# A graph network in one launch: the count codes made in other steps, and the check of the edge order taken off VectorE

## The chip, the cores and the metric

The kernel runs on one core of a Trainium2 chip. The metric is the device time of one execution in microseconds (us); a time of the kernel is the median of several runs. The engines are named as the profile names them: PE (TensorE; PEld are its weight loads), DVE (VectorE), ACT (ScalarE), POOL (GpSimd) and SP (SyncE, which here only starts transfers).

## The reference

```python
h = jnp.maximum(_layernorm(x, axis=-1), 0.0)      # x: 6250 nodes x 256
def agg(h):                                       # 100,000 edges src -> dst, sorted by dst
    return jax.ops.segment_sum(h[src], dst, num_segments=N)
for l in range(3):
    h = x + agg(x)                                # here x is the layer's input
    h = relu(h @ W1s[l] + b1s[l]); h = relu(h @ W2s[l] + b2s[l])
    x = h @ W3s[l] + b3s[l]
h = x + agg(x)                                    # the head has cW1, cW2 (256 to 64), cW3
out = x_in + (relu(relu(h @ cW1 + cb1) @ cW2 + cb2) @ cW3 + cb3)
```

So there are four aggregations, each a sum of neighbours' rows, and a small dense network behind each.

## The kernel before, in words

The 6250 nodes make 49 tiles of 128. An aggregation is done for most of its work as a dense product: the adjacency counts are built once as matrices of small integers (`mats`, built by `build` with the matmuls of line 1254 from the two one-hot factors of line 1200), and every layer multiplies them with the node features (line 1937, `agg<-a,XY`). A part of the nodes, those of low degree, is summed by gathering rows one per edge (line 1622, on POOL's queue).

Ahead of all this stands a **preparation**, whose instructions are put out in an order that the Python code fixes (a manual schedule), by generators that a driver loop steps on in turn. Three of them matter here.

- `normed` does the layer norm and the first product, `z = relu(norm(x)) @ W1`, for the 49 tiles in 25 pairs (0 to 24; the last has one tile). It is a pipeline over steps s. In step s, in this order: `out(s-3)` copies the product of pair s-3 from PSUM to `zs` on DVE (line 1053), `high(s-4)` rounds it into `XY` on ACT (line 1058), `scale(s)` makes the normed rows `h` on ACT (line 1025), `turn(s-1)` transposes them on PE (`agg<-ident,h`, line 1034) and copies the result to `ht` on ACT (line 1037), `times(s-2)` multiplies on PE (`bp<-w,ht`, line 1046), and `low(s-4)` takes the rest `zs - XY` on POOL (line 1063; five of the pairs on DVE). `keep(s-5)` stores `zs` (SP). The products lie in two PSUM buffers, so the product of pair p can start only when `out(p-2)` has copied its buffer away.
- `look` finds the range of edges of each half tile, and near its end, in lines 823 to 850, does two things in one go: it turns the **count codes** `cT` (a field of 128 x 16 x 50 bf16 inside `clT`) into a place below 128 and a weight of 1 or 256 for an odd or even count (`odd`, written over `weigh`), and it makes the **check**: are the edges in order (`run`, 892 int32 a partition, compared with itself shifted by one), does a window hold all its edges, do the windows end in range. The findings go to the four columns of `wrong`; a matmul with ones adds them over the partitions (line 847), and two small DVE steps make the flag `good` of them, which the end of the program reads to choose a fallback.
- `ranking` sorts the nodes by degree, mostly on DVE (lines 892 to 977).

The driver counts half steps h of `normed` (two for each s) and steps `look` on after those in the tuple `LOOK`, whose last is 45: after the whole of step s = 22. There all of lines 823 to 850 is put out at once, behind `out(19)` and ahead of `turn(22)`. Each engine works its list strictly in that order.

Behind the preparation its memory is given back. The first instruction of the build, the ACT copy `pairs<-clT` (line 1188), waits for everything that used that memory, the last stores of `zs` among them.

Of the kernel before, what the change touches and what calls it, by code (L numbers as in the profile page):

```python
# [9 lines left out]
F32 = mybir.dt.float32  # L10
I32 = mybir.dt.int32
# [3 lines left out]
BF16 = mybir.dt.bfloat16  # L15
AF = mybir.ActivationFunctionType
OP = mybir.AluOpType
PSUM = bass.MemoryType.PSUM
DRAM = bass.MemoryType.DRAM
P = 128  # L20
# [400 lines left out]
def sorted_edges(  # L421
# [39 lines left out]
    nc = tc.nc  # L461
# [8 lines left out]
    GD = 4  # L470
    NSUB = 2 * NT
    GSUB = 64 // GD
    TWO = GD // 2
    HW = NT * TWO
    STEP = 64
# [7 lines left out]
    EC = 892  # L483
# [8 lines left out]
    U = NT - NS  # L492
# [50 lines left out]
    cT, weigh, loT = clT[:, 0], clT[:, 1], clT[:, 2]  # L543
# [149 lines left out]
    def look(pool):  # L693
# [5 lines left out]
        run = pool.tile([P, EC + 1], I32, name="run", bufs=1)  # L699
        nc.gpsimd.memset(run, FAR)  # L700
        both = pool.tile([P, EC], I32, name="both", bufs=1)
        nc.gpsimd.memset(both, 0)
        for e, t, m in ((dst, run, EC + 1), (src, both, EC)):
# [18 lines left out]
                                       op1=OP.bitwise_or)  # L722
# [8 lines left out]
        for h in range(2):  # L731
# [5 lines left out]
                                    op0=OP.is_lt, op1=OP.add, accum_out=half[:NSUB, h:h + 1])  # L737
# [6 lines left out]
        near_i = pool.tile([P, NEAR], I32, name="near_i", bufs=1)  # L744
# [18 lines left out]
        less = pool.tile([P, GSUB + 1], F32, name="less", bufs=1)  # L763
        junk2 = near_i.bitcast(BF16)[:, :NEAR]
        DV = 11
        for k in range(GSUB + 1 - DV):
            for q in range(2 * k, min(2 * k + 2, DV)):
                nc.vector.tensor_scalar(junk[:NSUB], near[:NSUB], float(GD * q), None,  # L768
                                        op0=OP.is_lt, op1=OP.add, accum_out=less[:NSUB, q:q + 1])
            q = DV + k  # L770
            nc.scalar.activation(junk2[:NSUB], near[:NSUB], AF.Sign, bias=edge[:NSUB, q:q + 1],
                                 accum_out=less[:NSUB, q:q + 1])
            yield
        nc.vector.tensor_scalar(less[:NSUB, DV:], less[:NSUB, DV:], -0.5, float(NEAR // 2),
                                op0=OP.mult, op1=OP.add)
# [20 lines left out]
        for q0 in range(0, GSUB, H):  # L796
# [4 lines left out]
            hi = pool.tile([P, H, P], I32, name="hi", bufs=1)  # L801
            nc.vector.tensor_scalar(hi[:NSUB], wd[:NSUB, cut, :], 7, None,
                                    op0=OP.arith_shift_right)
# [5 lines left out]
            for t, o in ((r, cT), (f, loT)):  # L809
                for i in range(0, H, 4):  # L810
# [6 lines left out]
                    if t is r:  # L817
# [2 lines left out]
            yield  # L820


        odd = weigh[:, :, :2 * U]
        nc.vector.tensor_scalar(odd, cT[:, :, :2 * U], float(2 * STEP), -1.0, op0=OP.is_ge,
                                op1=OP.mult)
        for t in range(1, GD, 2):
            nc.vector.scalar_tensor_tensor(odd, cT[:, :, :2 * U], float(t * STEP), odd,
                                           op0=OP.is_ge, op1=OP.add)
        nc.vector.scalar_tensor_tensor(cT[:, :, :2 * U], odd, float(-STEP), cT[:, :, :2 * U],
                                       op0=OP.mult, op1=OP.add)  # L830
        nc.vector.tensor_scalar(odd, odd, 255.0, 1.0, op0=OP.mult, op1=OP.add)
        wrong = pool.tile([P, 4], F32, name="wrong", bufs=1)
        nc.vector.memset(wrong, 0.0)
        down = pool.tile([P, EC], F32, name="both", bufs=1)
        nc.vector.tensor_tensor(down, run[:, 1:EC + 1], run[:, :EC], OP.is_lt)
        nc.vector.tensor_reduce(wrong[:, 0:1], down, axis=mybir.AxisListType.X, op=OP.max)
        size = pool.tile([P, GSUB], F32, name="size", bufs=1)
        nc.vector.tensor_tensor(size[:NSUB], less[:NSUB, 1:], less[:NSUB, :GSUB], OP.subtract)
        nc.vector.tensor_scalar(size[:NSUB], size[:NSUB], float(P), None, op0=OP.is_gt)
        nc.vector.tensor_reduce(wrong[:NSUB, 1:2], size[:NSUB], axis=mybir.AxisListType.X,  # L840
                                op=OP.max)
        nc.vector.tensor_scalar(wrong[:NSUB, 2:3], less[:NSUB, GSUB:], float(NEAR), None,
                                op0=OP.is_ge)
        nc.vector.scalar_tensor_tensor(wrong[:NSUB, 2:3], first[:NSUB, GSUB:], float(E),
                                       wrong[:NSUB, 2:3], op0=OP.is_lt, op1=OP.mult)
        bad = ps_m.tile([P, W], F32, name="ps")
        nc.tensor.matmul(bad[:1, :4], ones[:, 0:1], wrong, start=True, stop=True)
        total = pool.tile([1, 1], F32, name="total", bufs=1)
# [5 lines left out]
    def stored_later(pool):  # L854

        zero = pool.tile([P, C], F32, name="b3b", bufs=1)
        nc.gpsimd.memset(zero, 0.0)
        yield
        for t in tables:
            nc.sync.dma_start(out=t[N:N + PAD, :], in_=zero)  # L860
        nc.sync.dma_start(out=padded[0:E].rearrange("(o e) -> o e", o=16),
                          in_=src.rearrange("(o e) -> o e", o=16))
        nc.sync.dma_start(out=padded[E:E + KR].rearrange("(o e) -> o e", o=1),
                          in_=src[E - KR:E].rearrange("(o e) -> o e", o=1))
        yield
# [224 lines left out]
            yield  # L1090

    sums = ps_g.tile([P, W], F32, name="sums")
    LOOK = tuple(range(17, 33, 2)) + (45,)
    RANK = tuple(range(33, 42))
    LATER = (14, 24)

    with tc.manual_schedule():
        with tc.tile_pool(name="prep", bufs=2) as prep, tc.tile_pool(
            name="ps_t", bufs=2, space=PSUM
        ) as ps_t, tc.tile_pool(name="ps_z", bufs=2, space=PSUM) as ps_z:  # L1100
            cN = prep.tile([P, 2 * NS, GSUB], BF16, name="cN", bufs=1)
            looked = look(prep)
            ranked = ranking(prep)
            next(looked)
            rows = normed(prep, ps_t, ps_z)
            next(rows)
            make_identity(nc, ident)
            nc.vector.tensor_copy(ident_r, ident)
            nc.vector.memset(eps, EPS)
            turn_biases, (b1, b2, b3) = load_biases(prep)  # L1110
            ahead_w = fused(prep, [W3s[l] for l in range(NLAYER)],
                            [W1s[l + 1] for l in range(NLAYER - 1)] + [cW1])
            next(ahead_w)
            next(looked)
            for t, pattern, base in ((cols[:, :U * TWO], [[1, U], [2 * STEP, TWO]], NS),
                                     (cols[:, U * TWO:], [[1, NS], [2 * STEP, TWO]], 0),
                                     (lanes, [[1, P]], 0), (colf, [[1, P]], 0)):
                nc.gpsimd.iota(t, pattern=pattern, base=base, channel_multiplier=0,
                               allow_small_or_imprecise_dtypes=True)
            next(looked)  # L1120
            next(rows)
            turn_biases()
            next(ranked)
            next(ranked)
            for k in range(2 * NLAYER):
                next(looked)
                next(ahead_w)
                if k == 0:
                    next(rows)
                next(rows)  # L1130
                next(rows)
            next(looked)
            stores = stored_later(prep)
            for h, _ in enumerate(rows, 4 * NLAYER):
                if h % 2:
                    ask(2)
                if h in LOOK:
                    next(looked)
                if h in RANK:
                    next(ranked)  # L1140
                if h in LATER:
                    next(stores)
            assert next(ranked, 0) == 0 and next(looked, 0) == 0 and next(stores, 0) == 0

        work = ctx.enter_context(tc.tile_pool(name="work", bufs=1))
# [827 lines left out]
        with tc.tile_pool(name="hots", bufs=1) as hots, tc.tile_pool(  # L1973
            name="ats", bufs=1
        ) as ats, tc.tile_pool(name="rings", bufs=AHEAD + 2) as rings, tc.tile_pool(
            name="gath", bufs=9
        ) as gath, tc.tile_pool(name="nd", bufs=1) as nd, tc.tile_pool(
            name="ps_a", bufs=2, space=PSUM
# [96 lines left out]
```

## Time and profile before

| | before |
|---|---|
| median of 3 runs (lowest to highest) | 2008.25 us (2006.13 to 2008.99) |
| the profiled execution: its time, its span | 2005.61 us, 2003.8 us |
| busy in the span: PE, PEld, DVE, ACT, POOL | 94%, 74%, 52%, 54%, 65% |
| chain that ended last: PE, DVE, DMA | 83%, 6%, 4% |
| preparation's last product ends, build begins | 130.5 us, 133.8 us |

The span runs from the first instruction to the last, and the 1.8 us between it and the execution's time lie around it. Starts in the profile are in us from the span's start. In a row of the timeline the first number is the start, the second how long the group took, and the bracket at the end, if there is one, tells how long the engine sat idle ahead of it and what ended that. In the rows of windows each engine's busy time stands ahead of the number of its instructions, and PEclk is the TensorE clock that was granted, as a share of full speed.

### The profile page before, as it was taken

The numbers are of one execution on the slowest core, as the hardware profiler recorded it, in microseconds if no ns is written. First come the engines' busy times: TensorE is split into PE (matmuls) and PEld (weight loads), VectorE is DVE, ScalarE is ACT, GpSimd is POOL, SyncE is SP. The second block draws the span as 40 slices with busy tenths as digits, with TensorE's granted clock in tenths as the row PEclk, the third lists the DMA queues.
The fourth block names the chain that finished last, engine by engine and source line by source line (L and its number), as shares of the span: only waits on it lengthen the run. The fifth ranks groups of instructions, "written<-read, shape, count | busy, mean of one in ns | idle before, by whom it ended". The sixth has DMA issues, their size and how long they took to land.

```text
span 2003.8 us, 29049 instructions
## 1 busy us (share of the span) xinstructions
PE 1885.4 (94%) x9236; PEld 1472.8 (74%) x9236; DVE 1034.1 (52%) x2213; ACT 1077.4 (54%) x2164; POOL 1311.1 (65%) x1444
## 2 busy tenths in 40 slices
PE   5955999999999899999999999999999999999997
PEld 3734766777777787777789777777788877777775
DVE  7877887677756343333344353333345354343433
ACT  4734776776766564444445464444445564455442
POOL 2526666766766556777777466676777466777775
PEclk9876999999999999999999999999999999999999
DMA  5523656665656475555656575564657576565553
GB/s 167 176 74 115 201 176 197 203 210 183 206 187 212 155 241 163 173 182 162 185 169 206 168 248 168 159 198 149 187 168 230 160 216 202 184 200 171 180 176 106
DMA packets 252333, 361.40 MB, mean 180 GB/s; under 512 B 33352, under 2 KB 206312, under 8 KB 252154
## 3 DMA queue, kind: packets, MB, share of 16 engines
q1 hardware_dynamic: 188160, 190.34, 30.0%
q0 software_dynamic: 61952, 166.87, 27.5%
q10 hardware_dynamic: 2058, 2.25, 0.4%
q8 instruction: 74, 1.21, 0.3%
q14 instruction: 89, 0.73, 0.1%
HBM read 292.33 MB, written 67.40 MB: 180 GB/s over the span
## 4 chain that ended last, share of the span: by engine, by line
PE 83%; DVE 6%; DMA 4%; issue 2%; POOL 2%; ACT 1%; SPq 0%; DVEq 0%; ACTq 0%; POOLq 0%
PE agg L1937 66%; PE ps L1514 6%; PE ps L1417 6%; DMA rows<-table,idxN 2%; PE bp L1254 2%; POOL rows L1622 1%; DVE hi L1200 1%; PE pt L1685 1%; PE bp L1046 1%; DVE lo L1200 1%; POOL lane L1743 1%; PE ps L1431 1%; DMA wd<-joined,starts 0%; DVE ws L768 0%; DMA lane<-padded,at 0%
## 5 line engine op out<-in xcount | busy, mean ns | idle before, releaser
L1937 PE MATMUL agg<-a,XY 128*128 128x512 f32 (+1 forms) x6272 | 1513.1, 393 | 15.4 <-DVE a L1910 6.9
L1622 POOL DMA_INDIRECT rows<-table,idxN x1121 | 1087.1, 970 | 473.9 <-PE agg L1937 211.0
L1937 PEld LDWEIGHTS agg<-a,XY 128*128 128x128 f32 x6272 | 1146.7, 189 | 249.2 <-issue 12.7
L1908 ACT CAST a<-at 128x512 fp32r<-128x512 uint8 (+1 forms) x1249 | 709.4, 602 | 237.9 <-PE agg L1937 226.8
L1658 DVE TENSOR_TENSOR sums<-sums,rows 128x512 f32<-128x512 f32 x477 | 332.1, 696 | 499.6 <-DMA rows<-table,idxN 444.8
L1910 DVE CAST a<-at 128x512 fp32r<-128x512 uint8 (+1 forms) x312 | 141.7, 460 | 171.4 <-PE agg L1937 147.8
L1262 ACT CAST at<-bp 128x392 uint16<-128x392 f32 x227 | 110.3, 489 | 128.0 <-PE bp L1254 122.2
L1417 PE MATMUL ps<-h,w 128*128 128x512 f32 (+2 forms) x336 | 135.3, 546 | 0.0
L1514 PE MATMUL ps<-w,h 128*128 128x256 f32 x588 | 133.7, 379 | 0.0
L1200 DVE TENSOR_TENSOR lo<-lanes,pairs 128x512 bf16<-128x512 bf16 x256 | 107.1, 424 | 45.1 <-PE bp L1254 44.3
L1254 PEld LDWEIGHTS <-lo 128*128 128x128 bf16 x1028 | 57.5, 103 | 96.8 <-DVE lo L1200 41.9
L1254 PE MATMUL bp<-hi,lo 128*128 128x98 bf16 x1028 | 95.2, 219 | 33.4 <-DVE lo L1200 27.1
L1514 PEld LDWEIGHTS ps<-w,h 128*128 128x128 f32 x588 | 111.2, 190 | 15.9
L596 POOL DMA_INDIRECT table<-zz,ids x72 | 72.9, 1013 | 66.3 <-DVE zz L1519 48.1
L1654 ACT COPY sums<-rows 128x512 f32<-128x512 f32 x74 | 43.8, 593 | 122.5 <-DMA rows<-table,idxN 101.1
L1420 ACT ACTIVATE h<-ps,bias 128x512 f32<-128x512 f32 (+2 forms) x84 | 51.7, 636 | 95.1 <-PE ps L1417 95.1
L1417 PEld LDWEIGHTS ps<-h,w 128*128 128x128 f32 x336 | 63.0, 193 | 52.6 <-issue 37.8
L1519 DVE TENSOR_TENSOR zz<-ps,w 128x512 f32<-128x512 f32 (+1 forms) x81 | 50.5, 639 | 96.0 <-PE ps L1514 89.3
L1693 ACT ACTIVATE h<-pt,bias 128x256 f32<-128x256 f32 (+1 forms) x84 | 33.1, 446 | 124.3 <-PE pt L1685 124.2
L1344 DVE TENSOR_TENSOR XY<-back,XY 128x256 fp32r<-128x256 f32 x138 | 55.1, 423 | 46.9 <-ACT XY L1343 46.0
L1951 ACT ACTIVATE h<-agg,bias 128x512 f32<-128x512 f32 (+1 forms) x60 | 37.6, 671 | 73.3 <-PE agg L1937 73.1
L1200 DVE TENSOR_TENSOR hi<-hi,pairs 128x784 bf16<-128x784 bf16 x128 | 72.6, 568 | 4.4
(235 smaller groups left out, 952.0 us busy)
## 6 DMA issues: line engine op xcount, KB each, us to landing
at<-mat SPq DMA_DIRECT2D x140, 448.0 KB
mat<-at SPq DMA_DIRECT2D x32, 784.0 KB
at<-mat SPq DMA_DIRECT2D x62, 336.0 KB
rows<-table,idxN POOLq DMA_INDIRECT x1121
back<-table SPq DMA_DIRECT2D x138, 128.0 KB
table<-zz SPq DMA_DIRECT2D x35, 256.0 KB
at<-mat SPq DMA_DIRECT2D x63, 112.0 KB
own<-zz SPq DMA_DIRECT2D x55, 128.0 KB
```

What stands on the lines that cost most here:

```text
L596: got = nc.gpsimd.indirect_dma_start(out=ap, out_offset=bass.IndirectOffsetOnAxis(ap=ids[:, b:b + 1], axis=0), in_=sb, in_offset=None)
L1200: nc.vector.tensor_tensor(o, values, which[:, :, None, :].to_broadcast(shape), op)
L1254: mm = nc.tensor.matmul(bp[:, m * HW:(m + 1) * HW], lo[:, m, :], hi[:, m, :], start=(i == 0), stop=(i == len(sets) - 1))
L1262: nc.scalar.copy(o, v)
L1344: later(1, lambda: nc.vector.tensor_tensor(XY[:, j:j + m, C:], z[:, :m, :], XY[:, j:j + m, :C].bitcast(F32), OP.subtract))
L1417: mm = nc.tensor.matmul(ps[:, :w], weights[l][0][:, c, i * P:(i + 1) * P], h1[:, c, :w], start=(c == 0), stop=(c == KC - 1))
L1514: mm = nc.tensor.matmul(o, h2[0][:, c, nodes], w3[:, c, :], start=(c == 0), stop=(c == KC - 1))
L1622: got = nc.gpsimd.indirect_dma_start(out=t[:, c % 2, :], out_offset=None, in_=tables[self.l][:, :], in_offset=bass.IndirectOffsetOnAxis(ap ...
L1658: nc.vector.tensor_tensor(sums, sums, rows.rearrange("p h c -> p (h c)"), OP.add)
L1908: nc.scalar.copy(o, v)
L1910: nc.vector.tensor_copy(o, v)
L1937: mm = nc.tensor.matmul(agg[c][:, :w], XY[:, j, o:o + P], a[:, :w], start=(i == 0 and half == 0), stop=(i == NT - 1 and half == 1))
```

## The change

Four things change, all in the preparation.

1. The codes are made of seven DVE steps in place of five: four `tensor_scalar` and three `tensor_tensor`, none of which takes a scalar and two tensors at once. The result is the same. One of them writes a small tile of its own (`upper`, under the name `hi`).
2. The edge order is checked by a subtraction on POOL (`rise`) and a Relu on ACT that adds up the falls, in place of a comparison and a reduction on DVE. The clearing of `wrong` and the subtraction `size` go to POOL as well.
3. `look` yields twice more. `LOOK` ends in (43, 45): the codes come a step earlier, behind `out(18)`; the check stays behind step 22.
4. The product with `wrong` and the two steps that make `good` come behind the whole of `normed`.

```diff
-        odd = weigh[:, :, :2 * U]
-        nc.vector.tensor_scalar(odd, cT[:, :, :2 * U], float(2 * STEP), -1.0, op0=OP.is_ge,
+        code, odd = cT[:, :, :2 * U], weigh[:, :, :2 * U]
+        nc.vector.tensor_scalar(odd, code, float(2 * STEP), float(-2 * STEP), op0=OP.is_ge,
                                 op1=OP.mult)
-        for t in range(1, GD, 2):
-            nc.vector.scalar_tensor_tensor(odd, cT[:, :, :2 * U], float(t * STEP), odd,
-                                           op0=OP.is_ge, op1=OP.add)
-        nc.vector.scalar_tensor_tensor(cT[:, :, :2 * U], odd, float(-STEP), cT[:, :, :2 * U],
-                                       op0=OP.mult, op1=OP.add)
-        nc.vector.tensor_scalar(odd, odd, 255.0, 1.0, op0=OP.mult, op1=OP.add)
+        nc.vector.tensor_tensor(code, code, odd, OP.add)
+        upper = pool.tile([P, GSUB, 2 * U], BF16, name="hi", bufs=1)
+        nc.vector.tensor_scalar(upper, odd, -1.0, None, op0=OP.mult)
+        nc.vector.tensor_scalar(odd, code, float(STEP), float(-STEP), op0=OP.is_ge, op1=OP.mult)
+        nc.vector.tensor_tensor(code, code, odd, OP.add)
+        nc.vector.tensor_tensor(code, code, upper, OP.add)
+        nc.vector.tensor_scalar(odd, odd, -255.0 / STEP, 1.0, op0=OP.mult, op1=OP.add)
+        yield
         wrong = pool.tile([P, 4], F32, name="wrong", bufs=1)
-        nc.vector.memset(wrong, 0.0)
-        down = pool.tile([P, EC], F32, name="both", bufs=1)
-        nc.vector.tensor_tensor(down, run[:, 1:EC + 1], run[:, :EC], OP.is_lt)
-        nc.vector.tensor_reduce(wrong[:, 0:1], down, axis=mybir.AxisListType.X, op=OP.max)
+        nc.gpsimd.memset(wrong, 0.0)
+        rise = pool.tile([P, EC], I32, name="both", bufs=1)
+        nc.gpsimd.tensor_tensor(rise, run[:, 1:EC + 1], run[:, :EC], OP.subtract)
+        rest = near_i.bitcast(BF16)[:, :EC]
+        nc.scalar.activation(rest, rise, AF.Relu, scale=-1.0, accum_out=wrong[:, 0:1])
         size = pool.tile([P, GSUB], F32, name="size", bufs=1)
-        nc.vector.tensor_tensor(size[:NSUB], less[:NSUB, 1:], less[:NSUB, :GSUB], OP.subtract)
+        nc.gpsimd.tensor_tensor(size[:NSUB], less[:NSUB, 1:], less[:NSUB, :GSUB], OP.subtract)
...
+        yield
         bad = ps_m.tile([P, W], F32, name="ps")
         nc.tensor.matmul(bad[:1, :4], ones[:, 0:1], wrong, start=True, stop=True)
...
-    LOOK = tuple(range(17, 33, 2)) + (45,)
+    LOOK = tuple(range(17, 33, 2)) + (43, 45)
...
+            next(looked)
             assert next(ranked, 0) == 0 and next(looked, 0) == 0 and next(stores, 0) == 0
```

Lines behind the change are 1 to 5 higher in the changed kernel: line 1053 is 1057 there, 1034 is 1038, 1046 is 1050, 1063 is 1067, 847 is 851. On DVE, before, near the end of the preparation (`zs<-bp` are the copies of `out`, here of pairs 18 and 19; the rows on `clT` are the codes, the rest is the check):

```order
L977 CAST what<-bits 128x24x3
L1053 COPY zs<-bp 128x512 x2
L824 TENSOR_SCALAR clT<-clT 128x16x50
L827 SCALAR_TENSOR_TENSOR clT<-clT 128x16x50 x2
L829 SCALAR_TENSOR_TENSOR clT<-clT 128x16x50
L831 TENSOR_SCALAR clT<-clT 128x16x50
L833 MEMSET wrong 128x4
L835 TENSOR_TENSOR both<-run 128x892
L836 TENSOR_REDUCE wrong<-both 128x1
L838 TENSOR_TENSOR size<-less 98x16
L839 TENSOR_SCALAR size<-size 98x16
L840 TENSOR_REDUCE wrong<-size 98x1
```

The same place on DVE in the changed kernel:

```order
L981 CAST what<-bits 128x24x3
L1057 COPY zs<-bp 128x512
L824 TENSOR_SCALAR clT<-clT 128x16x50
L826 TENSOR_TENSOR clT<-clT 128x16x50
L828 TENSOR_SCALAR hi<-clT 128x800
L829 TENSOR_SCALAR clT<-clT 128x16x50
L830 TENSOR_TENSOR clT<-clT 128x16x50
L831 TENSOR_TENSOR clT<-clT,hi 128x16x50
L832 TENSOR_SCALAR clT<-clT 128x16x50
L1057 COPY zs<-bp 128x512
L842 TENSOR_SCALAR size<-size 98x16
L843 TENSOR_REDUCE wrong<-size 98x1
```

The codes now stand between `out(18)` and `out(19)`, four rows of the check are gone from DVE, and the two steps that make `good` follow only behind `out(24)`.

On PE, before, the last products of the norm (`agg<-ident,h` is `turn`, `bp<-w_0_131,ht` is `times`) and the check's product among them; the two rows ahead of it are `turn(21)` and `times(20)`:

```order
L1034 MATMUL agg<-ident,h 128x128 x4
L1046 MATMUL bp<-w_0_131,ht 128x256 x4
L847 MATMUL ps<-wrong,ones 1x4
L1034 MATMUL agg<-ident,h 128x128 x4
L1046 MATMUL bp<-w_0_131,ht 128x256 x4
L1034 MATMUL agg<-ident,h 128x128 x4
L1046 MATMUL bp<-w_0_131,ht 128x256 x4
L1034 MATMUL agg<-ident,h 128x128 x2
L1046 MATMUL bp<-w_0_131,ht 128x256 x6
```

And in the changed kernel, the same rows from `turn(21)` on:

```order
L1038 MATMUL agg<-ident,h 128x128 x4
L1050 MATMUL bp<-w_0_131,ht 128x256 x4
L1038 MATMUL agg<-ident,h 128x128 x4
L1050 MATMUL bp<-w_0_131,ht 128x256 x4
L1038 MATMUL agg<-ident,h 128x128 x4
L1050 MATMUL bp<-w_0_131,ht 128x256 x4
L1038 MATMUL agg<-ident,h 128x128 x2
L1050 MATMUL bp<-w_0_131,ht 128x256 x6
L851 MATMUL ps<-wrong,ones 1x4
```

The check's product has gone behind the last `times`. On POOL, before, the end of the preparation is an unbroken row of `low` steps, with the gathers of the next stage behind:

```order
L994 MEMSET xs 128x256
L1063 TENSOR_TENSOR XY<-zs,XY 128x2x256 x12
L1063 TENSOR_TENSOR XY<-zs,XY 128x256
L1743 DMA lane<-padded,at 128x20 x4
L1743 DMA lane<-padded,at 128x17 x4
```

In the changed kernel:

```order
L998 MEMSET xs 128x256
L1067 TENSOR_TENSOR XY<-zs,XY 128x2x256 x7
L835 MEMSET wrong 128x4
L837 TENSOR_TENSOR both<-run 128x892
L841 TENSOR_TENSOR size<-less 98x16
L1067 TENSOR_TENSOR XY<-zs,XY 128x2x256 x5
L1067 TENSOR_TENSOR XY<-zs,XY 128x256
L1748 DMA lane<-padded,at 128x20 x4
```

The three new rows stand behind `low(18)` and ahead of `low(19)`. On ACT the new Relu stands in the same step, behind the copy `ht` of pair 21 and ahead of `high(19)`; it waits for the subtraction on POOL. SP's list does not change.

## Prediction

> **What bounds the kernel now.** I read the page's chain first, then the windows, to see in which stage this change lies and whether that stage is on the path.
>
> ```profile
> PE 83%; DVE 6%; DMA 4%; issue 2%; POOL 2%; ACT 1%; SPq 0%; DVEq 0%; ACTq 0%; POOLq 0%
> ...
> 100.00:134.00 34.00, 19.47 (x96) 15.51 (x94) 24.12 (x47) 14.33 (x30) 12.68 (x10) 0.90 0.21 69
> ...
> 300.00:400.00 100.00, 99.58 (x551) 70.38 (x550) 72.08 (x148) 70.90 (x146) 67.02 (x71) 1.00 0.63 200
> ```
>
> The whole program is bound by PE (99.6 us busy in 100 from 300 us on), but the changed stage is not: between 100 and 134 us PE is busy for 19.5 of 34 us. So a microsecond won there moves the start of a long PE-bound stretch, and counts in full if nothing else holds that start. The chain in order of time says what holds it:
>
> ```profile
> 112.26 0.68 DVE zs L1053
> 112.94 0.29 DVE clT L824
> 113.25 1.96 DVE clT L827
> 115.24 1.96 DVE clT L827
> 117.22 1.01 DVE clT L829
> ...
> 118.62 1.01 DVE both L835
> 119.66 1.08 DVE wrong L836
> 121.74 1.04 PE agg L1034 x4
> ...
> 131.46 1.72 DMA table<-zs
> 133.81 0.28 ACT pairs L1188
> 134.11 0.58 DVE hi L1200
> ```
>
> From 112.9 to 121.5 us the path lies on DVE, first on the codes, then on the check; then it goes through PE's last norm products, the last store and into the build without a break. PE's own rows show the cost:
>
> ```profile
> 112.49 1.97 PE L1046 MATMUL bp<-w,ht 128*128 128x256 f32 x8 [3.34 <-DVE zs L1053]
> 121.55 0.19 PE L847 MATMUL ps<-wrong,ones 128*1 128x4 f32 x2 [7.10 <-DVE wrong L844]
> 121.67 1.11 PE L1034 MATMUL agg<-ident,h 128*128 128x128 f32 x4
> 122.58 2.97 PE L1046 MATMUL bp<-w,ht 128*128 128x256 f32 x8
> 125.39 0.60 PE L1034 MATMUL agg<-ident,h 128*128 128x128 f32 x4
> 125.83 1.89 PE L1046 MATMUL bp<-w,ht 128*128 128x256 f32 x8
> ```
>
> Behind `times(20)`, which ends at 114.46, PE sits for 7.1 us for the check's product, with `turn(22)` queued behind it although its rows `h` are ready at 114.0. And the first products afterwards are slow: `bp` takes 2.97 in place of 1.89.
>
> **The change, step by step.** What goes: PE's wait for `wrong`. With the product at the end, `turn(22)` runs right behind `times(20)`, at about 114.5. What is late next is `times(21)`: its PSUM buffer comes free with `out(19)`, and `out(19)` now stands behind the codes on DVE. In the kernel before it stood ahead of them and cost nothing.
>
> When do the codes end? They start behind `out(18)`, at 112.26 in place of 112.86. Their price by kind:
>
> ```profile
> 112.86 0.36 DVE L824 TENSOR_SCALAR clT<-clT 128x800 bf16<-128x800 bf16 x1
> ...
> L1200 DVE TENSOR_TENSOR hi<-hi,pairs 128x784 bf16<-128x784 bf16 x128 | 72.6, 568 | 4.4
> ```
>
> Four one-tensor steps at 0.36 and three two-tensor steps of nearly the size of line 1200's at 0.57 make 3.15 us alone. (The upper bound of a two-tensor step on this field is line 829's 1.0: then 4.4.) Before, the five steps took 5.7 us, though alone they would be 2 x 0.36 + 3 x 1.0 = 3.7. The other 2 us are POOL's:
>
> ```profile
> 113.07 1.28 POOL L1063 TENSOR_TENSOR XY<-zs,XY 128x512 fp32r<-128x512 f32 x1 [5.69 <-ACT XY L1058]
> 115.06 1.28 POOL L1063 TENSOR_TENSOR XY<-zs,XY 128x512 fp32r<-128x512 f32 x1 [0.71 <-ACT XY L1058]
> ...
> 60.62 0.69 DVE L804 TENSOR_TENSOR rel<-hi,node 98x512 f32<-98x512 int32 x1
> ...
> 68.65 2.04 DVE L804 TENSOR_TENSOR rel<-hi,node 98x512 f32<-98x512 int32 x1
> ...
> 68.85 1.28 POOL L1063 TENSOR_TENSOR XY<-zs,XY 128x512 fp32r<-128x512 f32 x1
> ...
> 100.18 1.77 POOL L1063 TENSOR_TENSOR XY<-zs,XY 128x512 fp32r<-128x512 f32 x1 [2.58 <-ACT XY L1058]
> ```
>
> Each line 827 step runs beside one POOL `low` and ends 0.85 us after it: 114.35 to 115.20, 116.34 to 117.19. At 68.65 a DVE step that takes 0.69 at 60.62 takes 2.04 beside another `low`. So a two-tensor POOL step holds DVE's SBUF steps off until it is done (the copies `zs`, from PSUM, keep their 0.68 beside one).
>
> That is the price of the check on POOL. The subtraction has 892 elements where `low` has 512: 1.28 x 892 / 512 = 2.23 us, and it needs nothing but POOL, so it starts right behind `low(18)`, at 114.4 to 114.7, in the middle of the codes. (Bounds, as no POOL row has two int32 tensors: 0.84, what a POOL fill of 892 int32 takes in the row below, and twice the float rate, 4.5.) Then the codes wait for `low(18)`, 1.28, and the subtraction, 2.23: 112.26 + 3.15 + 1.28 + 2.23 = 118.9, less some 0.2 of overlap. `out(19)` then ends near 119.4. If DVE were held by `low(18)` alone, it would be 116.6 and 117.2. I take 119.4: both rows above show POOL taking its turn between two dependent DVE steps. The small POOL steps (`wrong`, `size`) are bounded by the second row here, 0.3 each.
>
> ```profile
> 1.53 0.84 POOL L702 MEMSET both<- 128x892 int32 x1
> ...
> 3.43 0.30 POOL L718 TENSOR_SCALAR edge<-edge 128x17 f32<-128x17 f32 x1
> ```
>
> The Trainium skill, in "GPSIMD Engine Reference", section "3.1 Elementwise — side-by-side cycle accounting", gives 4497 ns for a POOL `tensor_tensor` of 2048 fp32 and calls VectorE about twice as fast. By that the subtraction is an estimate of 1.96 us, 0.27 less than by the row, and the move to POOL speaks against itself: line 835 did its comparison on DVE in 1.08 us.
>
> The Relu is a new wait on ACT: it waits for POOL until about 116.9 and has `high(19)`, `scale(23)` and the copy `ht` of pair 22 queued behind it. Its price lies under the 1.47 + 0.20 us that the summing activation below takes for 1408 elements: some 1.1. It ends near 118.0, before `out(19)` at 119.4, so those wait for the codes anyway and it costs nothing. With `out(19)` at 117.2 this cover is gone, and ACT goes on from 118.0.
>
> ```profile
> 42.61 1.47 ACT L771 ACTIVATE near_i<-near,edge 98x1408 bf16<-98x1408 f32 x1
> 43.98 0.20 ACT L771 ACTIVATION_READ_ACCUMULATOR near_i<-near,edge 98x1 f32 x1
> ...
> 112.38 0.62 ACT L1058 CAST XY<-zs 128x512 fp32r<-128x512 f32 x1 [4.71 <-DVE zs L1053]
> 112.90 1.10 ACT L1025 ACTIVATE h<-xs,shift,rstd 128x256 f32<-128x256 f32 x2
> 113.90 0.57 ACT L1037 COPY ht<-agg 128x512 f32<-128x512 f32 x1
> ```
>
> From 119.4: `high(19)`, `scale(23)`, `ht(22)` on ACT follow at the spacing of these rows: `h` at 120.95, `ht` at 121.45. On PE `times(21)` starts at 119.55 (before: 122.58). DVE's rest of the check, 0.7 us, and `out(20)` end at 120.8, in time for `times(22)`. How long `times(21)` takes hangs on the clock:
>
> ```profile
> 112.50:114.50 2.00, 1.96 (x8) 1.40 (x8) 1.97 (x3) 2.00 (x5) 1.28 (x1) 1.00 0.63 211
> ...
> 121.50:125.40 3.90, 3.85 (x15) 3.22 (x16) 0.92 (x3) 1.61 (x3) 1.26 (x1) 0.58 0.22 74
> ...
> 135.80:140.00 4.20, 1.83 (x20) 1.59 (x20) 4.10 (x10) 1.34 (x4) 0.00 (x0) 0.50 0.25 92
> ...
> 127.78 2.75 PE L1046 MATMUL bp<-w,ht 128*128 128x256 f32 x12
> 135.82 0.81 PE L1254 MATMUL bp<-hi,lo 128*128 128x98 bf16 x8 [5.29 <-DVE lo L1200]
> ```
>
> After PE's 3.3 us of idleness (ahead of 112.49) the granted clock stays 1.00, after the 5.3 us that end at 135.8 it is 0.50, after 7.1 us 0.58. PE would now be idle from 115.0 (`turn(22)` done) to 119.55, 4.5 us: nearer to 5.3, so I take the slow clock. `times(21)` then takes its 2.81 of before to the next `turn`, and `times(22)` starts at 119.55 + 2.81 + 0.44 = 122.8; at full clock (1.73) it would be 121.7. The Trainium skill ("TensorE: Matmul & The Clock Gate", "Part 1: The HAM clock gate") has the clock halve after an idle window of about 3.4 us; by that it is the slow case too, -3.0, and not -4.1.
>
> From `times(22)` on, PE, ACT and DVE do what they did from 125.83 on. **The sum: 122.8 - 125.8 = -3.0 us.** The product with `wrong` and the steps of `good`, some 0.8 us behind the last `times`, are hidden by the last store, which ends 3.3 us after that product (130.5 to 133.8); without that cover they would cost the 0.8. Everything behind 133.8 follows by data, so I let it move along. The profiled execution took 2005.61 us, of which 2003.8 are its span: 2002.6 after. It lay 2.6 under the median, so for the median 2008.25 - 3.0 = **2005.2 us**.
>
> **The rivals.**
> - *The clock stays.* The idle gap is shorter than I reckon, or the slow state misses it: -4.1, 2004.1.
> - *DVE keeps its turn* (POOL gets none until the codes end, or the int32 subtraction takes 0.84): `out(19)` ends at 117.2, ACT goes on from 118.0 behind the Relu, `ht(22)` is there at 120.0, `times(22)` at 120.05: -5.8, 2002.5. For it: at 100.18 a `low` took 1.77, so POOL waits at times. Against it: both rows of line 827.
> - *A dear subtraction.* At 4.5 us DVE and ACT come 2.3 us later: -0.7, 2007.5.
> - *Slower.* The subtraction on POOL holds DVE and the Relu, and with them PE. It eats the gain at 2.23 + 3.0 = 5.2 us. At four times the float rate, 8.9 us and with the codes' other steps dearer (1.3), the sum is -3.0 + 6.7 + 1.3 = +5, 2013. No row shows int32 on POOL that slow; the fill speaks against it.
> - *It does not carry.* The preparation ends earlier, but the build's start or layer 0's is held by something that did not move: 0, 2008.2. The unbroken chain at 133.8 speaks against it.
>
> **How the numbers follow.** Forecast 0.46, clock stays 0.17, DVE keeps its turn 0.20, dear subtraction 0.07, does not carry 0.04, slower 0.06. The bound of 0.2% is 4.0 us, about what a measurement of this kernel can tell from no change. Faster by more: clock stays and DVE keeps its turn, and 0.04 of the forecast, as the runs of before lie up to 2.1 us under their median: 0.41. Slower by more: 0.06. Within: 0.53. The range goes from 2002.5 less 1.7 for that scatter to the case that does not carry with 0.8 for the scatter above the median: 2000.8 to 2009.0.
>
> **What would show it.** `turn(22)` close behind `times(20)`; the codes broken by POOL's subtraction of about 2.2 us and `out(19)` ending near 119.4; the Relu done before that; a `times(21)` at nearly 3 us; the last store's end and `pairs<-clT` near 130.8. I am wrong if the subtraction is far from 2.2 us, if DVE is not held, or if `pairs<-clT` moves by another amount than the end of the span.

## The result, and the profile after

| | before | after |
|---|---|---|
| median (lowest to highest) | 2008.66 us (2006.13 to 2009.06, 7 runs) | 2000.27 us (1998.64 to 2003.95, 7 runs) |
| ratio, 95% interval | | 0.9967 [0.9957, 0.9977] |
| profiled execution: time, span | 2005.61, 2003.8 us | 1999.98, 1998.2 us |
| `out(18)` starts | 111.66 | 111.02 |
| first `hi` of the build starts | 134.11 | 130.20 |

The changed kernel is faster by 6.6 us (4.6 to 8.6). Two more timings on other chips, told below, gave 0.9972 and 0.9971; the three weighted together are 0.9970, give or take 0.0006, or 6.0 us of 2007, give or take 1.2. Forecast were 3.0.

I use one measure all through: **the stretch** from the start of `out(18)` on DVE to the first `hi` of the build. It holds all the steps that the change moves and leaves out what stands ahead of them and behind. It took 22.45 us before and 19.18 after.

DVE's timeline of the changed kernel in that stretch (start, duration, group, and in brackets the idle time ahead of it):

```profile
111.02 0.68 DVE L1057 COPY zs<-bp 128x512 f32<-128x512 f32 x1
111.62 0.36 DVE L824 TENSOR_SCALAR clT<-clT 128x800 bf16<-128x800 bf16 x1
112.01 0.58 DVE L826 TENSOR_TENSOR clT<-clT 128x800 bf16<-128x800 bf16 x1
112.50 1.48 DVE L828 TENSOR_SCALAR hi<-clT 128x800 bf16<-128x800 bf16 x1
114.02 1.71 DVE L829 TENSOR_SCALAR clT<-clT 128x800 bf16<-128x800 bf16 x1
115.76 0.58 DVE L830 TENSOR_TENSOR clT<-clT 128x800 bf16<-128x800 bf16 x1
116.37 0.58 DVE L831 TENSOR_TENSOR clT<-clT,hi 128x800 bf16<-128x800 bf16 x1
116.86 0.36 DVE L832 TENSOR_SCALAR clT<-clT 128x800 bf16<-128x800 bf16 x1
117.14 0.69 DVE L1057 COPY zs<-bp 128x512 f32<-128x512 f32 x1
```

The four one-tensor steps (`TENSOR_SCALAR`) are alike, and two of them take four times as long as the others. POOL and ACT at that time say why:

```profile
112.43 1.29 POOL L1067 TENSOR_TENSOR XY<-zs,XY 128x512 fp32r<-128x512 f32 x1 [5.69 <-ACT XY L1062]
113.67 0.09 POOL L835 MEMSET wrong<- 128x4 f32 x1
113.72 1.78 POOL L837 TENSOR_TENSOR both<-run 128x892 int32<-128x892 int32 x1
115.47 0.32 POOL L841 TENSOR_TENSOR size<-less 98x16 f32<-98x16 f32 x1
...
115.53 0.95 ACT L839 ACTIVATE near_i<-both 128x892 bf16<-128x892 int32 x1 [1.72 <-POOL both L837]
116.39 0.19 ACT L839 ACTIVATION_READ_ACCUMULATOR near_i<-both 128x1 f32 x1
```

Line 828 ends (113.98) just after `low(18)` (113.72), line 829 (115.73) just after the subtraction (115.50). The Relu is done at 116.6, before `out(19)` starts at 117.14. PE's rows of the changed kernel:

```profile
111.84 3.45 PE L1050 MATMUL bp<-w,ht 128*128 128x256 f32 x8 [3.33 <-DVE zs L1057]
115.09 0.84 PE L1038 MATMUL agg<-ident,h 128*128 128x128 f32 x4
117.97 2.77 PE L1050 MATMUL bp<-w,ht 128*128 128x256 f32 x8 [2.04 <-DVE size L842]
120.54 1.06 PE L1038 MATMUL agg<-ident,h 128*128 128x128 f32 x4
121.40 2.39 PE L1050 MATMUL bp<-w,ht 128*128 128x256 f32 x8
123.62 0.38 PE L1038 MATMUL agg<-ident,h 128*128 128x128 f32 x2
123.84 2.76 PE L1050 MATMUL bp<-w,ht 128*128 128x256 f32 x12
126.53 0.19 PE L851 MATMUL ps<-wrong,ones 128*1 128x4 f32 x2
```

The wait of 7.1 us for the check has become one of 2.0 us for `out(19)`, and `times(22)` starts at 121.40 in place of 125.83. The end of the stretch, from the chain of waits:

```profile
127.20 0.15 DVE good L854
...
127.52 1.74 DMA table<-zs
...
129.90 0.28 ACT pairs L1193
130.20 0.58 DVE hi L1205
```

`good` is ready at 127.3, 2.6 us before the build begins: the last store still covers it. (The chain names `good` ahead of that store, but the store starts 0.41 us after `out(24)` ends, as it does in the kernel before, at 0.42: `good` does not hold it.)

### The profile page after: what moved, and what is told of

Its sections match the earlier page's. It is cut to its first block, busy times and chain, and to the rows that moved or that the text cites. A ratio compares the mean times of both kernels' runs of the same rounds, so it can differ in the third digit from the quotient of the medians.

```text
span 1998.2 us, 29053 instructions
## 1 busy us (share of the span) xinstructions
PE 1883.4 (94%) x9236; PEld 1471.0 (74%) x9236; DVE 1030.9 (52%) x2211; ACT 1075.0 (54%) x2166; POOL 1309.6 (66%) x1447
## 4 chain that ended last, share of the span: by engine, by line
PE 82%; DVE 7%; DMA 5%; issue 3%; POOL 2%; ACT 1%; SPq 0%; DVEq 0%; ACTq 0%; POOLq 0%
PE agg L1942 64%; PE ps L1519 6%; PE ps L1422 6%; DMA rows<-table,idxN 3%; PE bp L1259 2%; PE bp L1050 1%; DVE ws L768 1%; DVE hi L1205 1%; POOL rows L1627 1%; PE pt L1690 1%; POOL lane L1748 1%; DVE lo L1205 1%; PE ps L1436 1%; PE ps L1482 0%; ACT a L1913 0%
```

## The experiments

All ratios are against the kernel before on the same chip. A diff shows the edit against the kernel that the heading names, with `...` where lines are left out. Theory one is the prediction's: the time moves by what the stretch moves. The rivals differ from case to case.

**The kernel before again.** No edit.

> The kernel before once more, unchanged. The changed kernel's profile has pairs<-clT 3.9 us earlier than before (129.90 against 133.81), 0.64 of it already ahead of the first changed instruction, and its span 5.6 us shorter; the ratio of the times is 6.6 us. Theory one (the time follows the stage one to one, the rest is scatter between executions): ratio 1.000 within 0.001, but this profile may differ from the first one by 1 to 2 us in the same places (start of the copies behind the ranking, pairs<-clT to the first aggregated rows at 235.8). Theory two (an earlier start of the build is worth more than itself): this profile agrees with the first one to 0.3 us at both places, and the 1.7 us lost behind pairs<-clT are due to the change.

Ratio 0.9998 [0.9989, 1.0008]. Its stretch took 23.27 us, 0.8 more than in the first profile. PE's rows of this second profile of before show one cause:

```profile
112.41 3.49 PE L1046 MATMUL bp<-w,ht 128*128 128x256 f32 x8 [3.32 <-DVE zs L1053]
121.46 0.19 PE L847 MATMUL ps<-wrong,ones 128*1 128x4 f32 x2 [5.56 <-DVE wrong L844]
121.58 1.11 PE L1034 MATMUL agg<-ident,h 128*128 128x128 f32 x4
122.49 3.62 PE L1046 MATMUL bp<-w,ht 128*128 128x256 f32 x8
125.91 0.82 PE L1034 MATMUL agg<-ident,h 128*128 128x128 f32 x4
```

The same `times(20)` behind the same 3.3 us of idleness took 1.97 there and 3.49 here, and `times(21)` 2.97 and 3.62. So a stretch is known to some 0.8 us, and 22.9 is the mean for before. From the first `hi` to the first aggregated rows (the `h` made from `agg`) this profile needs 101.8 us, the first one of before 101.7, that of after 100.5. Theory two asked for agreement to 0.3 us there and at the start of the copies; both hold (`out(18)` starts at 111.58 and 111.66), so this run by itself leaned to theory two. The two later profiles of after, told below, take that back for this segment.

**The kernel before with only its product behind the norm.**

```diff
+        yield
         bad = ps_m.tile([P, W], F32, name="ps")
...
+            next(looked)
             assert next(ranked, 0) == 0 and next(looked, 0) == 0 and next(stores, 0) == 0
```

> Only the product with wrong and the two steps of good go behind the norm; codes and check stay as before on DVE. Theory one (PE's wait for the product is what the change removes): PE goes on with turn(22) and times(21) at 114.5, since out(19) stands ahead of the codes here; the next wait is times(22) for out(20), behind the whole DVE block, at about 122.2 in place of 125.8: pairs<-clT near 130.2, the time 3.6 us under before. Rival (the cheaper codes are the gain): DVE's block still ends at 121.4, so 0 to -1 us.

Ratio 0.9988 [0.9979, 0.9997], stretch 20.67 us: 2.2 us under before's mean, where 3.6 were expected. PE's rows:

```profile
116.31 0.60 PE L1035 MATMUL agg<-ident,h 128*128 128x128 f32 x4
116.75 1.89 PE L1047 MATMUL bp<-w,ht 128*128 128x256 f32 x8
118.48 0.60 PE L1035 MATMUL agg<-ident,h 128*128 128x128 f32 x4
122.75 3.58 PE L1047 MATMUL bp<-w,ht 128*128 128x256 f32 x8 [3.67 <-DVE zs L1054]
```

PE does go on with `times(21)`, and then waits 3.7 us for `out(20)`, which stands behind the whole DVE block. `times(22)` starts at 10.6 us from `out(18)` (before: 14.2), as expected; but it runs at the slow clock, 3.58 in place of 1.89, and that takes back the rest.

**The kernel before with only its codes in seven steps**, at the old place.

```diff
-        odd = weigh[:, :, :2 * U]
-        nc.vector.tensor_scalar(odd, cT[:, :, :2 * U], float(2 * STEP), -1.0, op0=OP.is_ge,
+        code, odd = cT[:, :, :2 * U], weigh[:, :, :2 * U]
+        nc.vector.tensor_scalar(odd, code, float(2 * STEP), float(-2 * STEP), op0=OP.is_ge,
                                 op1=OP.mult)
...
+        nc.vector.tensor_scalar(odd, odd, -255.0 / STEP, 1.0, op0=OP.mult, op1=OP.add)
         wrong = pool.tile([P, 4], F32, name="wrong", bufs=1)
```

> Only the codes are made by the seven steps, at the old place and with the old check and product. Theory one: alone 3.15 us against 3.7, and two of POOL's low steps still hold them, so 5.7 becomes about 5.1: everything behind moves by 0.6 us, within the noise of the time. Rival (three-operand steps are what POOL holds, two-operand steps slip through): the codes take 3.2 us, -2.5 us.

Ratio 1.0000 [0.9991, 1.0009]; the stretch 22.43. The rival falls: the two-tensor and one-tensor steps are held as well, and the codes take 5.2 us (111.04 to 116.24), 0.5 less than before. DVE's rows:

```profile
111.44 1.54 DVE L826 TENSOR_TENSOR clT<-clT 128x800 bf16<-128x800 bf16 x1
112.91 0.35 DVE L828 TENSOR_SCALAR hi<-clT 128x800 bf16<-128x800 bf16 x1
113.29 1.45 DVE L829 TENSOR_SCALAR clT<-clT 128x800 bf16<-128x800 bf16 x1
```

**The kernel before with only its check on POOL and ACT**, everything else at its old place.

```diff
-        nc.vector.memset(wrong, 0.0)
-        down = pool.tile([P, EC], F32, name="both", bufs=1)
-        nc.vector.tensor_tensor(down, run[:, 1:EC + 1], run[:, :EC], OP.is_lt)
-        nc.vector.tensor_reduce(wrong[:, 0:1], down, axis=mybir.AxisListType.X, op=OP.max)
+        nc.gpsimd.memset(wrong, 0.0)
+        rise = pool.tile([P, EC], I32, name="both", bufs=1)
+        nc.gpsimd.tensor_tensor(rise, run[:, 1:EC + 1], run[:, :EC], OP.subtract)
+        rest = near_i.bitcast(BF16)[:, :EC]
+        nc.scalar.activation(rest, rise, AF.Relu, scale=-1.0, accum_out=wrong[:, 0:1])
...
```

> The kernel before with only the edge check taken to POOL and ACT; codes, their place and the product's place as before. From out(18) to the build's first hi (22.5 and 23.3 us in the two profiles of before): the old codes are held by low(18) and by the subtraction (1.8 us) and end about 1 us later than before, the check behind them takes 0.7 us in place of 3, so the product stands 1.2 us earlier. Theory one (the time follows this stretch): -1.2 us. Theory three (a check on POOL and ACT gives some 2.5 us that the stretch does not show, as the changed kernel's two timings and the one with the late build suggest against the three kernels without it): -3.7 us.

This, the next and one more ran on a chip where the kernel before took 2180.81 us, at a mean granted clock near 0.95 in place of 0.975, so their ratios are wide. Ratio 0.9994 [0.9973, 1.0016]; the stretch 22.25, 0.6 us under before's mean, where 1.2 were expected. As a time it tells nothing apart. But the sharing of POOL and DVE goes both ways, as POOL's row shows: the subtraction took 2.38 us here; as it came at 113.00, a DVE step of the old codes was under way, which ended at 113.85.

```profile
113.00 2.38 POOL L835 TENSOR_TENSOR both<-run 128x892 int32<-128x892 int32 x1
```

**The changed kernel with its check on DVE.**

```diff
-        nc.gpsimd.memset(wrong, 0.0)
-        rise = pool.tile([P, EC], I32, name="both", bufs=1)
-        nc.gpsimd.tensor_tensor(rise, run[:, 1:EC + 1], run[:, :EC], OP.subtract)
-        rest = near_i.bitcast(BF16)[:, :EC]
-        nc.scalar.activation(rest, rise, AF.Relu, scale=-1.0, accum_out=wrong[:, 0:1])
+        nc.vector.memset(wrong, 0.0)
+        down = pool.tile([P, EC], F32, name="both", bufs=1)
+        nc.vector.tensor_tensor(down, run[:, 1:EC + 1], run[:, :EC], OP.is_lt)
+        nc.vector.tensor_reduce(wrong[:, 0:1], down, axis=mybir.AxisListType.X, op=OP.max)
...
-        nc.gpsimd.tensor_tensor(size[:NSUB], less[:NSUB, 1:], less[:NSUB, :GSUB], OP.subtract)
+        nc.vector.tensor_tensor(size[:NSUB], less[:NSUB, 1:], less[:NSUB, :GSUB], OP.subtract)
```

> The changed kernel with its edge check back on DVE (clearing, comparison, reduction, size), at the same place. Theory one (POOL's subtraction holds the codes for 1.8 us): the codes run on after low(18), out(19) ends near 116.1 in place of 117.8, the check then takes 2.9 us and out(20) ends near 119.7, so times(22) starts near 119.8 in place of 121.6: about 1.9 us under the changed kernel, 5 or more under before. Rival (taking the check off DVE is part of the gain): 1 to 2 us over the changed kernel, since DVE does 2.4 us more work.

Ratio 0.9974 [0.9964, 0.9985], stretch 17.82 us: 1.4 under the changed kernel's, where 1.9 were expected. DVE's rows:

```profile
112.62 1.46 DVE L828 TENSOR_SCALAR hi<-clT 128x800 bf16<-128x800 bf16 x1
114.11 0.37 DVE L829 TENSOR_SCALAR clT<-clT 128x800 bf16<-128x800 bf16 x1
...
115.90 0.68 DVE L1056 COPY zs<-bp 128x512 f32<-128x512 f32 x1
```

With the subtraction off POOL, line 829 takes 0.37 in place of 1.71; line 828, beside `low(18)`, keeps its 1.46. That shows the hold, and that in the stretch the move of the check to POOL costs 1.4 us on balance (one profile here against three of the changed kernel). The time does not show it: 5.2 us under before (3.0 to 7.2), not apart from the changed kernel's 6.0.

**The codes behind `out(19)`.**

```diff
-        yield
         wrong = pool.tile([P, 4], F32, name="wrong", bufs=1)
...
-    LOOK = tuple(range(17, 33, 2)) + (43, 45)
+    LOOK = tuple(range(17, 33, 2)) + (45,)
```

> The changed kernel with its codes one copy later: behind out(19), together with the check. Theory one (out(19) behind the codes is the wait that took the place of the old one): times(21) starts right behind turn(22), the next gate is out(20), behind the codes (held 3.1 us by POOL) and 0.7 us of check, at 8.6 us after the start of out(18); times(22) there in place of 10.4 to 10.9: from out(18) to the first hi 17.2 to 17.6 us against 19.2, the time 1.7 us under the changed kernel. Rival (the clock and ACT set the pace, not out(19)): the stretch stays at 19.

Stretch 17.56 us, as expected; ratio 0.9980 [0.9964, 0.9996], on the slower chip. PE's rows (`out(18)` starts at 113.63 here):

```profile
117.74 0.60 PE L1037 MATMUL agg<-ident,h 128*128 128x128 f32 x4
118.17 1.89 PE L1049 MATMUL bp<-w,ht 128*128 128x256 f32 x8
...
122.81 1.97 PE L1049 MATMUL bp<-w,ht 128*128 128x256 f32 x8 [1.36 <-DVE zs L1056]
```

`times(21)` follows `turn(22)` without a wait, and the next gate is `out(20)`: `times(22)` starts 9.2 us after `out(18)` began, where 8.6 were expected. So moving the codes ahead of `out(19)`, as the change does, costs 1.6 us in the stretch.

**The changed kernel in small pieces.** Codes and check on DVE, in pieces between `out(20)` and `out(24)`, the rest behind.

```diff
         nc.vector.tensor_tensor(code, code, odd, OP.add)
+        yield
         upper = pool.tile([P, GSUB, 2 * U], BF16, name="hi", bufs=1)
...
         nc.vector.tensor_scalar(odd, code, float(STEP), float(-STEP), op0=OP.is_ge, op1=OP.mult)
+        yield
         nc.vector.tensor_tensor(code, code, odd, OP.add)
         nc.vector.tensor_tensor(code, code, upper, OP.add)
+        yield
         nc.vector.tensor_scalar(odd, odd, -255.0 / STEP, 1.0, op0=OP.mult, op1=OP.add)
...
+        nc.vector.tensor_tensor(down, run[:, 1:EC + 1], run[:, :EC], OP.is_lt)
+        yield
+        nc.vector.tensor_reduce(wrong[:, 0:1], down, axis=mybir.AxisListType.X, op=OP.max)
...
-    LOOK = tuple(range(17, 33, 2)) + (43, 45)
+    LOOK = tuple(range(17, 33, 2)) + (45, 47, 49, 51)
```

> The changed kernel with all of codes and check on DVE, but in pieces of about 1 us between the copies out(20) to out(24), the reduction and the rest of the check behind out(24), the product behind all. Theory one (PE waits only for out(19) and out(20); DVE has some 1.3 us free in each step of the pipeline): from out(18) to the build's first hi 14.5 to 16.5 us, against 19.2 in the changed kernel and 17.8 with the check on DVE in one piece: 6 to 8 us under before, ratio 0.9965 within 0.001. Rival (POOL's low steps hold the pieces and so each copy out, or the check behind out(24) outlasts the last store): 18 us or more, no better than the changed kernel.

Ratio 0.9959 [0.9947, 0.9971], 8.2 us under before; stretch 15.42 us, as expected. PE's rows:

```profile
112.08 1.97 PE L1051 MATMUL bp<-w,ht 128*128 128x256 f32 x8 [3.34 <-DVE zs L1058]
113.88 0.60 PE L1039 MATMUL agg<-ident,h 128*128 128x128 f32 x4
114.31 1.89 PE L1051 MATMUL bp<-w,ht 128*128 128x256 f32 x8
116.04 0.60 PE L1039 MATMUL agg<-ident,h 128*128 128x128 f32 x4
116.48 1.89 PE L1051 MATMUL bp<-w,ht 128*128 128x256 f32 x8
...
125.66 0.19 PE L852 MATMUL ps<-wrong,ones 128*1 128x4 f32 x2 [3.88 <-DVE wrong L849]
```

PE runs through the last products with no gap but one of 0.35 us ahead of the last, `times` takes 1.9 to 2.0 us throughout, and PE is done by 121.8. What is late now is the check itself: its product comes 3.9 us later, and the build waits for `good`:

```profile
126.37 0.44 ACT L1194 COPY pairs<-clT 128x96 bf16<-128x96 bf16 x2 [3.00 <-DVE good L855]
```

This version beats the kernel before; against the changed kernel, timed beside it at 0.9972 [0.9961, 0.9983], its stretch is 3.8 us shorter, while the intervals of the two ratios still meet.

**The changed kernel, its build held back by six idle steps**, and **by four**, the latter twice.

```diff
         nc.vector.tensor_scalar(good, total, 0.0, None, op0=OP.is_equal)
+        for _ in range(6):
+            nc.vector.tensor_tensor(rise, run[:, 1:EC + 1], run[:, :EC], OP.subtract)
```

> The changed kernel with six more subtractions of 892 int32 on DVE behind the two steps of good (6 us, needed by nothing), so that pairs<-clT waits until about 133.5, where it stands in the kernel before; all else is the change. Theory one (the time follows the end of the preparation one to one): the whole gain is gone, ratio 1.000 within 0.001. Theory two (something of the gain does not come through the preparation's end): the ratio stays under 0.9985.

> The changed kernel with four idle subtractions on DVE behind good, in place of six, which lasted 8 us since POOL held them. The stretch from out(18) to the first hi should come to 22.9 to 23.9 us, as in the kernel before (22.5 and 23.3). Theory one: ratio 1.000 within 0.001. Theory three (some 2.5 us of the gain come from elsewhere): 0.9988 or less.

> The changed kernel with four idle subtractions behind good once more; its first timing had an interval of 0.2% either way. The stretch was 22.5 us, as in the kernel before. Theory one: ratio 1.000 within 0.001. Theory three: 0.9988 or less.

With six: ratio 0.9999 [0.9990, 1.0007], stretch 26.05. The rows of the idle steps and of the two `low` steps beside them:

```profile
128.73 8.04 DVE L856 TENSOR_TENSOR both<-run 128x892 int32<-128x892 int32 x6
128.70 3.77 POOL L1069 TENSOR_TENSOR XY<-zs,XY 128x512 fp32r<-128x512 f32 x2 [0.66 <-ACT XY L1064]
```

The steps lasted 8.0 us, not 6, since they and the last `low` steps (3.77 us here, 1.95 in the changed kernel) held each other, so the build began 3.2 us later after `out(18)` than before's mean and the time was still that of before. With four: stretch 22.51 and 22.52, ratio 0.9999 [0.9978, 1.0020] on the slower chip and 0.9988 [0.9979, 0.9997] on a usual one.

From the changed kernel to the one with six steps the stretch grows by 6.9 us and the time by 5.8 (from 6.0 below before to 0.2 below), give or take 2.1: the time does follow the stretch about one to one. But theory one's level is missed: with before's stretch the time lies 2.4 us lower (0.6 to 4.2), and with 3.2 us more it is equal.

**The changed kernel twice more.** No edit.

> The changed kernel once more, unchanged. From the start of out(18) to the first hi of the build it took 19.2 us in its first profile; the kernel before took 22.5 and 23.3 in its two, so the stage gives 3.3 to 4.1 us, while the ratio of the first seven runs gave 6.6 with an interval from 4.6 to 8.6. Theory one (the time moves by what the stage gives): a ratio of 0.998, within 0.001. Theory two (an earlier build is worth more than itself): a ratio of 0.9967 again.

> The changed kernel a third time, since two timings gave 6.6 and 5.6 us where the stretch from out(18) to the build's first hi became shorter by 3.3 to 4.1 in the profiles. Theory one (the rest is scatter: single executions of one kernel lie up to 3 us from their median): 0.998 within 0.001. Theory three (some 2 us more come from elsewhere): 0.997.

Ratios 0.9972 [0.9961, 0.9983] and 0.9971 [0.9961, 0.9981]; stretches 19.18 and 19.15. Both ratios lie inside theory one's band (0.997 to 0.999), at its far end, and at theory three's value: neither timing decides by itself. So the gain of the stretch is 3.7 us against before's mean, the same in three profiles, and the gain of the time is 6.0, give or take 1.2 (the stretch of before, known from two profiles 0.8 us apart, adds some 0.4 to the doubt when the two are compared). Their single profiled executions took 2004.54 and 2003.64 us, where the first took 1999.98: the part behind the first `hi` differs by 4 us between executions of one kernel. The segment from the first `hi` to the first aggregated rows took 101.85 and 101.79 us, so the 100.5 of the first profile was scatter.

| kernel | stretch, us | against 22.9 | ratio | time, us | time less stretch |
|---|---|---|---|---|---|
| before, again | 23.27 | | 0.9998 | -0.4 | |
| codes only | 22.43 | -0.5 | 1.0000 | 0.0 | +0.5 |
| product late | 20.67 | -2.2 | 0.9988 | -2.4 | -0.2 |
| check on DVE | 17.82 | -5.1 | 0.9974 | -5.2 | -0.1 |
| in small pieces | 15.42 | -7.5 | 0.9959 | -8.2 | -0.7 |
| after, three times | 19.2 | -3.7 | 0.9970 | -6.0 | -2.3 |
| six idle steps | 26.05 | +3.2 | 0.9999 | -0.2 | -3.4 |
| four idle steps, second | 22.52 | -0.4 | 0.9988 | -2.4 | -2.0 |

(Times are the ratios on 2007 us; each carries about 2 us either way, after's 1.2. The three kernels on the slower chip are left out.)

## Why the prediction was partly right

The sign was right, and the likeliest case, -3.0, missed the size: the first seven runs gave -6.6, three timings -6.0. A gain over 4.0 us had 0.41, a smaller change 0.53. Carried over by the ratio to the 2008.25 us that the forecast started from, the first result is 2001.6, near the low end of the range; its own median, 2000.27, beside a before of 2008.66, is under it. That low end allows 1.7 us for a scatter that the sentence ahead of it puts at 2.1, and no row gives the 1.7; with 2.1 it would be 2000.4.

*PE's wait goes, `times(21)` is late next.* Right: 7.1 us became 2.0 (1.5 to 2.3 in the three profiles of after), and what ended them was `out(19)` (the row names line 842, the DVE step that starts as `out(19)` ends). The kernel with the product alone shows the first half by itself, the one with the codes behind `out(19)` the second: without that new wait the stretch is 1.6 us shorter.

*POOL holds DVE.* Right in kind: line 829 at 1.71 with the subtraction on POOL and 0.37 without. The subtraction was overpriced, 1.78 us for 2.23: POOL's int32 goes at 2.0 ns per element, its float at 2.5. The figure of the Trainium skill ("GPSIMD Engine Reference", "3.1 Elementwise — side-by-side cycle accounting") led to an estimate of 1.96, nearer, though it is for fp32. The codes took 5.6 us (111.62 to 117.22) in place of some 6.5, and `out(19)` ended 6.8 us after `out(18)` began in place of 7.7.

*The Relu costs nothing.* Right: 1.14 us for the 1.1 reckoned, done 1.2 us before `out(19)` ends.

*The clock.* Wrong in the reading, near in the sum. I took from one row that 3.3 us of idleness leave the clock whole and reckoned that 4.5 halve it. PE's next idle time was 2.0 us only: `times(20)` itself ran slow, 3.45, behind the very 3.3 us after which it took 1.97 in before, and `out(19)` came 0.9 us earlier than forecast. (With six idle steps, where `times(20)` took 1.97, the idle time was 3.73.) Over all 14 profiles, that product was fast four times and slow ten, at the same idle time. The windows of the changed kernel show the clock of `times(20)` in the first row, of the wait in the second:

```profile
111.80:115.10 3.30, 3.26 (x9) 2.50 (x10) 3.23 (x4) 2.01 (x4) 2.67 (x3) 0.55 0.23 79
115.10:118.00 2.90, 0.86 (x6) 0.65 (x4) 2.80 (x7) 1.18 (x3) 0.69 (x2) 0.92 0.00 0
```

The Trainium skill ("TensorE: Matmul & The Clock Gate", "Part 1: The HAM clock gate") has the window of about 3.4 us run freely. The 1.97 and the 3.45 behind 3.3 us agree with that; that an idle time of about the window's length falls on either side by chance is my inference. From the start of `times(21)` to the next `turn` it was 2.57 us for the 2.81 reckoned, in the other two profiles of after 3.4.

*The sum in the stretch.* Forecast: -3.0. Measured: -3.7 against the mean of two profiles of before, -3.3 against the one that the forecast used. `pairs<-clT` starts 18.9 us after `out(18)`, for 19.1 forecast, and the steps of `good` are covered by the last store, as said. That the two come so close is in part luck: `out(19)` came 0.9 us earlier than forecast, which would have made it -3.9, and slower products behind it took 0.6 of that back (in the first profile `times(22)` at 2.39 for 1.89, in the other two `times(21)` at 3.6).

*The rest follows.* If a step failed, as far as is known it is this one: "Everything behind 133.8 follows by data, so I let it move along". In slope it holds (5.8 us of time for 6.9 of stretch). But some 2 us of the gain, 2.3 give or take 1.2 by the three timings of after, do not seem to lie in the stretch. The table shows them in all timings on the usual chips of kernels with the check on POOL and ACT, and in none of those without; no profile shows where they are. The part ahead of `out(18)` differs by up to 2.3 us between profiles and the part behind the first `hi` by 5.6, with no order by kernel: the five profiles on the usual chips with the check on POOL and ACT have means of 111.2 and 1869.9 us for the two parts, the six without 111.3 and 1870.1. So the profiles show 0.3 us of the 2.3; such a difference of means is known to some 2 us only. The sign that the prediction named, `pairs<-clT` against the end of the span, moved by 3.9 and 5.6 us, and is no better than that scatter. The run meant to tell, the check alone on POOL and ACT, fell on the slow chip. So that share **stays open**: a cause in the moved check is suggested by the pattern, not shown, and scatter is not excluded.

*The rivals.* "DVE keeps its turn" had a time, 2002.5, that would fit, but not its mechanism: POOL did take its turn, twice. "The clock stays" did not happen. "A dear subtraction" and "slower" fall with 1.78 us. "It does not carry" falls with the idle steps.

## What to carry to other kernels

When one engine's list waits for a flag that only the end needs, move the flag's step behind the list; but look at what the steps that make it are queued ahead of, since the next wait is theirs, and break them into pieces that fit the slack of the pipeline (here the stretch became shorter by 7.5 us in place of 3.7). Moving work from DVE to POOL can be no relief if both work from SBUF at that moment: here DVE's steps on SBUF waited for POOL's two-tensor step to end, and 0.37 us became 1.71. For a change of a few microseconds, compare one stretch across several profiles, and take the whole time from several timings, for a single profiled execution may lie 3 us from its kernel's median.

## What the hardware showed that I had not expected

- POOL's two-tensor subtraction of 892 int32 took 1.78 to 1.80 us in the profiles of after where nothing held it: 2.0 ns an element, against 2.5 for the float steps (1.28 us for 512).
- The hold is mutual: the same subtraction took 2.38 us where a DVE step was under way as it came, in the kernel with only its check moved. POOL's step of 98 x 16 took 0.32 us free and 0.95 us there.
- DVE's steps with one tensor are held as those with two: 0.36 becomes 1.48. The copies from PSUM are not: 0.69 beside a `low` at 120.84.
- Behind 3.3 us of PE idleness the clock came out either way: the same product of eight passes took 1.97 us in four profiles, 3.4 to 3.75 in nine and 3.08 in one.
